# Shorter runs in the memory layout of scratch, weights and inputs: a cross-attention and mixture-of-experts block on one Trainium2 core

## The chip, the core and the metric

One Trainium2 chip, of which the kernel uses one core. The metric is the device time in microseconds of one execution; the time of a kernel is the median of several runs. The engines are called TensorE (PE; its weight loads are PEld), VectorE (DVE), ScalarE (ACT), GpSimd (POOL) and SyncE (SP). DMA transfers are issued here from two queues: SP's (q1 in the profile, "hardware_dynamic") and POOL's (q0, "software_dynamic"). Both run on the same 16 DMA engines of the core.

## What is computed

`x` is (4, 512, 512), `ctx_1024` is (4, 512, 256), all float32. A cross-attention whose queries and keys come from the context is added to `x`, then a transformer block with 16-head causal attention and a mixture of experts (16 experts of width 352, the best 6 for each token, and one shared expert of width 704).

```python
def _L0_xattn_ref(teacher_logits, teacher_features, Wq, bq, Wk, bk):
    query = jnp.einsum('bnc,dc->bnd', teacher_features, Wq) + bq
    key = jnp.einsum('bnc,dc->bnd', teacher_features, Wk) + bk
    energy = jnp.einsum('bnd,bmd->bnm', query, key)
    attention = jax.nn.softmax(energy, axis=-1)
    return jnp.einsum('bln,bmn->blm', teacher_logits, attention)
...
    h = rmsnorm(x, ln1_w)
    q, k, v = h @ wq, h @ wk, h @ wv          # 16 heads of 128
    attn = softmax(causal(q k^T / sqrt(128)))
    x = x + (attn v) @ wo
    t = rmsnorm(x, ln2_w)
    probs = softmax(t @ gate_w.T); topv, topi = top_k(probs, 6); topv = topv / sum(topv)
    hh = silu(t eg_w^T) * (t eu_w^T)          # each expert
    out = x + sum_e cw_e (hh ed_w^T) + shared expert(t)
...
x = x + _L0_xattn_ref(_layernorm(x), ctx_1024, ...)
x = x + _L0_ffn_ref(_layernorm(x), ...)
```

(The second block is shortened to its formulas.)

## The kernel before

Every float32 matrix is split into a high and a low float16 part, and a product is three matmuls (`mm3`, L80 to L87). A tile has 128 partitions (rows); tokens go in four tiles of 128 per batch element, called "batch" here.

The work has three stages. The head (`xattn`, L204) is the cross-attention of one batch. It runs for batch 0 first, then mostly for batch 1; batches 2 and 3 are advanced in small steps (`bring`) between the heads of the second stage. For batches 0 and 1 its inputs are loaded from SP's queue, for batches 2 and 3 from POOL's (`feed`, L176). Weights of head 0 (`wqk0`) and group 0 (`wv0`) are loaded early from SP (L221).

The second stage goes over 64 pairs of batch and attention head in the order of `path`: `queries`, `values` (once for two heads), `scores`, `attend` one head later (`LAG`), `project` after each pair of heads. `scores` turns the softmax's result with a DMA transpose on SP's queue (`flip`, L90 and L91): `pt<-pn`, four a head, 256 in all. `attend` reads `pt`. Similar transposes are `ptp<-pn` and `hT<-hh` in the cross-attention and `h2T<-h2p` before the router.

`fetch` (L407) brings the weights of a head (`wqk`) or of a group of two heads (`wv`, `wo`). The first time it loads float32 into a staging tile (L423), splits it, and stores the split weights to a scratch tensor in memory (L429). Two neighbouring batches share a fetched tile (`partner`); for the other pair of batches the tile is fetched back from scratch (L414). Scratch stores and fetches are on POOL's queue, apart from the first head's store.

Other rows go to memory and back. (The profile leaves numbers out of names, so `x1_d` is `x_d` there.) The cross-attention stores its result `x1_d` (L339) and, for batches 2 and 3, its normed rows `hid_d` (L356), which `project` loads (L698). `rest_step` (L522) and `last_residual` reload `x1_d`, add, and store the residual `r_d`, which `residual` (L709) loads as the accumulator `acc` on SP's queue. `shared_weights` (L440, load at L451) loads the shared expert's weights piece by piece. `pad_rows` (L479) fills rows of the token buffer `xs_d` with zeros, once for each of 16 experts. The routed tokens are scattered into `xs_d` with indirect DMAs on POOL's queue (L467).

The third stage runs the shared expert and then 16 experts on the gathered tokens, with their weights from SP's queue (L939), outputs in `y_d`, and indirect gathers (`yg`) that add them to `acc`.

The order of the instructions on each engine is made at build by a planner with a simulated timeline; `after` (L93) adds an order between two instructions, `pin` keeps program order. Within a queue, instructions go in that order; the program states no order between queues except through the data.

Of the kernel before, what the change touches and what calls it, by code (L numbers as in the profile page):

```python
# [47 lines left out]
PS = 4096.0  # L48
GS = 8.0
LAG = 1  # L50
MLAG = 2
# [4 lines left out]
def xattn_moe_block_kernel(ctx: ExitStack, tc: tile.TileContext, x, xT, ctxT, wqkx, bqk, ln1, ln2,  # L56
# [23 lines left out]
    def mm3(o, terms, start=True, stop=True, hold=None):  # L80
        n = len(terms)
        for j, (lh, ll, rh, rl) in enumerate(terms):
            ins = nc.tensor.matmul(o, lh, rh, start=start and j == 0, stop=False)  # L83
            if hold and j == 0:
                after(ins, hold)
            nc.tensor.matmul(o, lh, rl, start=False, stop=False)  # L86
            ins = nc.tensor.matmul(o, ll, rh, start=False, stop=stop and j == n - 1)  # L87
        return ins

    def flip(o, i):  # L90
# [40 lines left out]

    hid_d = [dram.tile([P, NT, D], F32, name=f"hid_d{b}") for b in range(B)]
    x1_d = [dram.tile([P, NT, D], F32, name=f"x1_d{b}") for b in range(B)]
    wqk_d = [dram.tile([P, 2048], F16, name=f"wqk_d{h}") for h in range(H)]
    wv_d = [dram.tile([P, 8 * GW], F16, name=f"wv_d{g}") for g in range(G)]
    wo_d = [dram.tile([P, 2 * HG * D], F16, name=f"wo_d{g}") for g in range(G)]
    xs_d = dram.tile([ROWS, 2 * D], F16, name="xs_d")
    r_d = [dram.tile([P, NT, D], F32, name=f"r_d{b}") for b in range(B)]
    y_d = dram.tile([OFFS[E], D], F32, name="y_d")
# [39 lines left out]
    def ctx_load(b):  # L179
        t = stg.tile([P, 1024], F32, tag="st", name="ct32").rearrange("p (c s) -> p c s", c=CC)  # L180
        feed(b).dma_start(t, ctxT[b])
        return t

# [20 lines left out]
    def xattn(b):  # L204
        ct32 = ctx_load(b) if b else ct0

        def turned(j):
            t = (stg if b else wg).tile([P, 1024], F32, tag="st" if b else "wo", name="xT32")
            feed(b).dma_start(t, xT[b, j])
            return t  # L210
# [5 lines left out]
        if b == 0:  # L216
            nc.sync.dma_start(ln1b, ln1.partition_broadcast(P))
            for nm, src in (("wqk0", wqk[0]), ("wv0", wv[0])):
                t = vp.tile([P, NT, 2, GW], F16, tag="vt", name=f"{nm}_st")
                early_st[nm] = t.rearrange("p t a d -> p (t a d)").bitcast(F32)  # L220
                nc.sync.dma_start(early_st[nm], src)  # L221
        ctp = ap_.tile([P, 2, CC, S], F16, tag="lnp", name="ctp")
# [109 lines left out]
        for t in range(NT):  # L332
# [5 lines left out]
            q = nc.gpsimd if b else nc.sync  # L338
            q.dma_start(x1_d[b][:, t, :], xv)  # L339
            st = asm.tile([P, 6], F32, name="st")  # L340
# [14 lines left out]
            if b >= 2:  # L355
                q.dma_start(hid_d[b][:, t, :], hd)  # L356
            if stop == "A":
# [36 lines left out]
    def shared_pool():  # L394
        actx.close()
        sp = ctx.enter_context(tc.tile_pool(name="sp", bufs=1, side="right", reuse_waits="tile"))
        shx["p"] = ctx.enter_context(tc.tile_pool(name="ac0", bufs=1, side="right", reuse_waits="tile"))
        shw = shx["w"] = sp.tile([P, 2, C * 2 * SI], F16, name="shw")
        sdw = shx["d"] = sp.tile([P, 2, 6 * D], F16, name="sdw")
        for j in range(0, C * 2 * SI, 1024):  # L400
            pieces.append((shw[:, :, j:min(j + 1024, C * 2 * SI)], sgu[:, j:min(j + 1024, C * 2 * SI)]))
        for j in range(0, 6 * D, 1024):
            pieces.append((sdw[:, :, j:j + 1024], sd[:, j:j + 1024]))

    held, partner, seen = {}, {}, set()

    def fetch(b, g, pool, tag, n, src, scr, nm):  # L407
# [5 lines left out]
        if nm in seen:  # L413
            nc.gpsimd.dma_start(w.rearrange("p a n -> p (a n)"), scr)  # L414
            return w
        seen.add(nm)
        first = nm in early_st
        if first:
            st_ = early_st[nm]
        else:  # L420
            st_ = stg.tile([P, 1024], F32, tag="st", name=f"{nm}_st")
            q = nc.sync if nm == "wqk1" else nc.gpsimd
            ins = q.dma_start(st_[:, :n], src)  # L423
            if nm == "wqk1":
                after(ins, zz["hT", 0])
        for j, ins in enumerate(split(w[:, 0], w[:, 1], st_[:, :n], WS)):
            if first:
                after(ins, zz["nb"] if j else zz["calm"][0])
        ins = (nc.sync if nm == "wqk0" else nc.gpsimd).dma_start(scr, w.rearrange("p a n -> p (a n)"))  # L429
        if nm != "wqk0":  # L430
# [9 lines left out]
    def shared_weights():  # L440
# [6 lines left out]
        if pieces:  # L447
            dst, src = pieces.pop(0)
            n = src.shape[1]
            st_ = stg.tile([P, 1024], F32, tag="st", name="shst")[:, :n]  # L450
            pin(nc.gpsimd.dma_start(st_, src))  # L451
            loaded.append((dst, st_))
# [26 lines left out]
    def pad_rows(e):  # L479
        r = e * T + CAP + 1 - 3 * HB  # L480
        dst = xs_d[r:r + 3 * HB, :].rearrange("r d -> (r d)").rearrange("(p a n) -> p a n", p=P, a=2)
        src = causal[:, :S - P].bitcast(F16).unsqueeze(1).to_broadcast([P, 2, 2 * (S - P)])
        after(nc.gpsimd.dma_start(dst, src), zz["pad"])

    def route1(b, x2):
# [20 lines left out]
        if b == B - 1:  # L506
            pace(h2p[0:1, D:D + 1])
            for t, x1t in enumerate(x1s):
                after(nc.gpsimd.tensor_tensor(x1t, x1t, x2[:, t, :], ALU.add), scats[0])
                nc.gpsimd.dma_start(r_d[b][:, t, :], x1t)  # L510

    x1s = []

    def last_residual(b):
        for t, (pool, tag) in enumerate([(he, "pn3"), (he, "pn3"), (xp, "x1t"), (xp, "h2")]):
            x1t = pool.tile([P, D], F32, tag=tag, name="x1t", **({} if pool is he else dict(bufs=1)))
            nc.gpsimd.dma_start(x1t, x1_d[b][:, t, :])
            x1s.append(x1t)
# [3 lines left out]
    def rest_step():  # L522
        if rest:
            b, t, x2 = rest.pop(0)
            x1t = xp.tile([P, D], F32, tag="x1t", name="x1t", bufs=1)
            ins = nc.gpsimd.dma_start(x1t, x1_d[b][:, t, :])
            for s in scats[-1:]:
                after(ins, s)
            nc.gpsimd.tensor_tensor(x1t, x1t, x2[:, t, :], ALU.add)
            nc.gpsimd.dma_start(r_d[b][:, t, :], x1t)  # L530

# [163 lines left out]
    def project(b, g):  # L695
        if b not in x2s:
            x2s[b] = x2p.tile([P, NT, D], F32, tag="x2", name="x2")
            nc.gpsimd.dma_start(x2s[b], hid_d[b])  # L698
        ao, x2 = aos[b, g], x2s[b]
# [9 lines left out]
    def residual(b):  # L709
        if b not in accs:  # L710
            pool = hpool if b else shx["p"]
            accs[b] = pool.tile([P, NT, D], F32, tag="hT", name=f"acc{b}")
            nc.sync.dma_start(accs[b], r_d[b])
        return accs[b]
# [522 lines left out]
def host_layout(i):  # L1237
# [5 lines left out]
    r["x"] = f["x"]  # L1243
    r["xT"] = f["x"].transpose(0, 2, 1).reshape(B, 2, 2, P, S).transpose(0, 1, 3, 2, 4).reshape(B, 2, P, 2 * S)
    r["ctxT"] = f["ctx_1024"].transpose(0, 2, 1).reshape(B, CC, P, S).transpose(0, 2, 1, 3)
    r["wqkx"] = np.stack([_pc(f["L0_xattn_Wq"].T, CC), _pc(f["L0_xattn_Wk"].T, CC)], 1)
# [6 lines left out]
    for n in ("wqk", "wv", "wo"):  # L1253
        r[n] = r[n].reshape(r[n].shape[0], P, -1)
    r["gate"] = _pc(g("gate_w").T, C).reshape(P, C * E)
# [10 lines left out]
    cols.append(np.concatenate([sg[:, :, 5 * P:], su[:, :, 5 * P:]], 2).reshape(P, C * P))  # L1266
    r["sgu"] = np.concatenate(cols, 1)
    r["sd"] = _pc(np.pad(g("sd_w").T, ((0, 6 * P - SI), (0, 0))), 6).reshape(P, 6 * D)
    return {k: np.ascontiguousarray(v) for k, v in r.items()}
# [24 lines left out]
```

## Time and profile before

| | |
|---|---|
| median of 3 runs | 1773.08 us (1766.79 to 1774.21) |
| profiled execution, its own time | 1762.41 us |
| its span, first to last instruction | 1760.7 us |
| mean granted TensorE clock | 0.993 |
| bytes moved by DMA | 296.24 MB, 168 GB/s over the span |
| memory read, written | 124.81 MB, 88.94 MB |
| `wqk<-wqk_d`, POOL, 20 times 512 KB | 5.0 us from issue to landing (median) |
| `wqk_d<-wqk`, POOL, 15 times 512 KB | 4.0 us |
| `wqk_st<-in_wqk_dram`, POOL, 14 times 512 KB | 6.4 us |
| `xs_d<-causal`, POOL, 16 times 384 KB | 5.6 us |

The profile is of one execution. Its busy shares are averages over the span; its line of DMA digits gives, in 40 equal slices, the mean busy share of the 16 DMA engines in tenths. A row of a DMA issue has the line, the issuing queue, what is written from what, how many, KB each, and the median time from issue to landing. The duration of an issue on POOL's queue is the time in which POOL prepares the transfer, not the transfer itself. A row of the window view has start and end, length, then the busy time of each engine with its instructions, the granted clock, the DMA share and GB/s. The rows of the DMA queues have packets, MB, and the time that their packets took as a share of 16 engines over the window; packets that overlap can bring a share over 100%. Under the profile lie the trace's packet records, each with its queue, start, duration and size.

### The profile page before, as it was taken

The numbers are of one execution on the slowest core, as the hardware profiler recorded it, in microseconds if no ns is written. First come the engines' busy times: TensorE is split into PE (matmuls) and PEld (weight loads), VectorE is DVE, ScalarE is ACT, GpSimd is POOL, SyncE is SP. The second block draws the span as 40 slices with busy tenths as digits, with TensorE's granted clock in tenths as the row PEclk, the third lists the DMA queues.
The fourth block names the chain that finished last, engine by engine and source line by source line (L and its number), as shares of the span: only waits on it lengthen the run. The fifth ranks groups of instructions, "written<-read, shape, count | busy, mean of one in ns | idle before, by whom it ended". The sixth has DMA issues, their size and how long they took to land. (4 is left out here: it accounts for less than half of the span.)

```text
span 1760.7 us, 27659 instructions
## 1 busy us (share of the span) xinstructions
PE 1708.6 (97%) x9919; PEld 932.9 (53%) x9919; DVE 1116.2 (63%) x2766; ACT 829.3 (47%) x1711; POOL 485.1 (28%) x614
## 2 busy tenths in 40 slices
PE   7899999999998999999999999999999999999998
PEld 3555556565654555556555544455555555555553
DVE  6787877787785676776667647544434344356755
ACT  4565655565643545454445422344544445444431
POOL 5524212240255242121113454300000000034654
PEclk9999999999999999999999999999999999999999
DMA  7787867575687787556547653755554546589866
GB/s 246 181 205 184 225 150 192 122 196 118 138 183 187 163 177 179 120 120 118 111 104 132 140 155 128 247 173 148 150 173 137 154 143 163 154 228 254 221 198 213
DMA packets 392212, 296.24 MB, mean 168 GB/s; under 512 B 334880, under 2 KB 335136, under 8 KB 391296
## 3 DMA queue, kind: packets, MB, share of 16 engines
q1 hardware_dynamic: 353360, 159.87, 39.9%
q0 software_dynamic: 38704, 134.51, 25.5%
q8 instruction: 80, 1.31, 0.3%
q14 instruction: 68, 0.56, 0.1%
HBM read 124.81 MB, written 88.94 MB: 121 GB/s over the span
## 5 line engine op out<-in xcount | busy, mean ns | idle before, releaser
L1169 POOL DMA_INDIRECT yg<-y_d,yrc x96 | 109.9, 1145 | 505.2 <-PE u L87 426.0
L673 ACT ACTIVATE pe<-pe,bnm 128x128 f32<-128x128 f32 (+3 forms) x256 | 142.5, 557 | 161.5 <-DVE bnm L671 161.3
L83 PE MATMUL qk<-hT,wqk 128*128 128x512 f16 (+1 forms) x520 | 196.4, 378 | 9.1 <-DMA wqk<-wqk_d 5.5
L86 PE MATMUL qk<-hT,wqk 128*128 128x512 f16 (+1 forms) x520 | 196.5, 378 | 0.0
L87 PE MATMUL qk<-hT,wqk 128*128 128x512 f16 (+1 forms) x520 | 196.3, 377 | 0.0
L74 DVE SCALAR_TENSOR_TENSOR pn<-pe,brc,pn 128x128 f16<-128x128 f32 (+3 forms) x256 | 148.1, 590 | 21.3 <-ACT pn L73 18.0
L671 DVE CUSTOM_DVE_ANT_0 pe<-sc,causal 128x128 f32<-128x128 f32 (+3 forms) x256 | 117.0, 485 | 66.9 <-PE sc L668 65.9
L73 ACT ACTIVATE pn<-pe,brc 128x128 f16<-128x128 f32 (+3 forms) x256 | 133.5, 553 | 34.1 <-ACT pe L673 17.8
L83 PE MATMUL v<-wv,hT 128*128 128x256 f16 x512 | 139.8, 273 | 0.9 <-DMA hT<-hh 0.9
L87 PE MATMUL v<-wv,hT 128*128 128x256 f16 x512 | 139.7, 273 | 0.0
L86 PE MATMUL v<-wv,hT 128*128 128x256 f16 x512 | 139.7, 273 | 0.0
L83 PE MATMUL g<-xT,wt 128*128 128x384 f16 (+2 forms) x384 | 127.3, 331 | 0.0
L86 PE MATMUL g<-xT,wt 128*128 128x384 f16 (+2 forms) x384 | 127.2, 331 | 0.0
L87 PE MATMUL g<-xT,wt 128*128 128x384 f16 (+2 forms) x384 | 127.2, 331 | 0.0
L1058 ACT ACTIVATE hT_e<-hf 128x384 f16<-128x384 f32 (+3 forms) x96 | 51.1, 532 | 133.6 <-DVE hf L1072 133.2
L83 PE MATMUL y<-dt,hT_e 128*128 128x512 f16 (+1 forms) x288 | 109.4, 380 | 0.0
L87 PE MATMUL y<-dt,hT_e 128*128 128x512 f16 (+1 forms) x288 | 108.9, 378 | 0.0
L86 PE MATMUL y<-dt,hT_e 128*128 128x512 f16 (+1 forms) x288 | 108.9, 378 | 0.0
L73 ACT ACTIVATE qkt<-qk 128x512 f16<-128x512 f32 x128 | 75.1, 587 | 70.7 <-PE qk L87 70.5
L705 DVE SCALAR_TENSOR_TENSOR x<-wo,x 128x512 f32<-128x512 f32 x128 | 87.2, 685 | 33.3 <-PE wo L87 32.9
L467 POOL DMA_INDIRECT xs_d<-h2p,slotu x96 | 98.7, 1028 | 28.3 <-issue 27.1
L74 DVE SCALAR_TENSOR_TENSOR qkt<-qk,qkt 128x512 f16<-128x512 f32 x128 | 87.5, 684 | 18.3 <-ACT qkt L73 15.2
(333 smaller groups left out, 4041.5 us busy)
## 6 DMA issues: line engine op xcount, KB each, us to landing
y_d<-yt SPq DMA_DIRECT2D x96, 256.0 KB, 2.8
est<-in_ew_dram SPq DMA_DIRECT2D x32, 704.0 KB, 6.2
est<-in_ed_dram SPq DMA_DIRECT2D x16, 768.0 KB, 4.7
wqk<-wqk_d POOLq DMA_DIRECT2D x20, 512.0 KB, 5.0
wqk_d<-wqk POOLq DMA_DIRECT2D x15, 512.0 KB, 4.0
wqk_st<-in_wqk_dram POOLq DMA_DIRECT2D x14, 512.0 KB, 6.4
xs_d<-causal POOLq DMA_DIRECT2D x16, 384.0 KB, 5.6
wv<-wv_d POOLq DMA_DIRECT2D x10, 512.0 KB, 5.7
```

Source lines behind the costliest of these rows:

```text
L73: return (nc.scalar.activation(hi, src, AF.Copy, scale=scale), nc.vector.scalar_tensor_tensor(lo, src, scale, hi, ALU.mult, ALU.subtract))
L74: nc.vector.scalar_tensor_tensor(lo, src, scale, hi, ALU.mult, ALU.subtract))
L83: ins = nc.tensor.matmul(o, lh, rh, start=start and j == 0, stop=False)
L86: nc.tensor.matmul(o, lh, rl, start=False, stop=False)
L87: ins = nc.tensor.matmul(o, ll, rh, start=False, stop=stop and j == n - 1)
L467: ins = nc.gpsimd.indirect_dma_start(out=xs_d, out_offset=bass.IndirectOffsetOnAxis(ap=slotu[:, tt, k:k + 1], axis=0), in_=h2ps[tt], in_of ...
L671: nc.vector.tensor_tensor_reduce(pe, ps[:, :w], causal[:, S - w:], -1.0, 3e38, ALU.add, ALU.min, nm)
L673: nc.scalar.activation(pe, pe, AF.Exp, bias=nm, scale=-1.0, accum_out=sm)
L705: nc.vector.scalar_tensor_tensor(x2[:, t, :], ps, 1.0 / (VS * WS), x2[:, t, :], ALU.mult, ALU.add)
L1058: nc.scalar.activation(hT[:R, ic, :w], hf, AF.Copy)
L1169: nc.gpsimd.indirect_dma_start(out=yg, out_offset=None, in_=src, in_offset=bass.IndirectOffsetOnAxis(ap=idx[:, tt, k:k + 1], axis=0))
```

## The change

A helper `runs` issues a DMA in which the side in memory is blocked: its outer index counts runs, then come 128 partitions, then the run itself, so that one partition's row is made of runs that lie apart, and the same run of the 128 partitions lies together. The tile on chip keeps its layout. With `RUN = 256` float32 (512 float16) the scratch of the split weights (`wqk_d`, `wv_d`, `wo_d`), of the residual (`x1_d`, `r_d`) and of the normed rows (`hid_d`) has runs of 1 KB. A partition's 4 KB of split weights were one run; a token tile's 2 KB of `x1_d`, `r_d` or `hid_d` were one run of a row of 8 KB. The inputs `xT`, `ctxT`, `wqk`, `wv`, `wo` and the shared expert's `sgu` and `sd` are laid out on the host in runs of 2 KB instead of 4 KB. `pad_rows` writes three runs of 1 KB a partition instead of two of 1.5 KB. Queues, waits, tiles and the work of the engines are the same in the program's text.

```diff
+RUN = 256
...
+    def runs(q, o, i):
+        blocks = [v.rearrange("p (q n) -> p q n", q=w.shape[0]) if len(v.shape) == 2 else v.rearrange("q p n -> p q n")
+                  for v, w in ((o, i), (i, o))]
+        return q.dma_start(*blocks)
...
-    hid_d = [dram.tile([P, NT, D], F32, name=f"hid_d{b}") for b in range(B)]
-    x1_d = [dram.tile([P, NT, D], F32, name=f"x1_d{b}") for b in range(B)]
-    wqk_d = [dram.tile([P, 2048], F16, name=f"wqk_d{h}") for h in range(H)]
-    wv_d = [dram.tile([P, 8 * GW], F16, name=f"wv_d{g}") for g in range(G)]
-    wo_d = [dram.tile([P, 2 * HG * D], F16, name=f"wo_d{g}") for g in range(G)]
+    def rows_d(nm, b):
+        return dram.tile([NT, D // RUN, P, RUN], F32, name=f"{nm}{b}")
+
+    def weights_d(nm, i):
+        return dram.tile([2048 // (2 * RUN), P, 2 * RUN], F16, name=f"{nm}{i}")
+
+    hid_d, x1_d, r_d = ([rows_d(nm, b) for b in range(B)] for nm in ("hid_d", "x1_d", "r_d"))
+    wqk_d = [weights_d("wqk_d", h) for h in range(H)]
+    wv_d, wo_d = ([weights_d(nm, g) for g in range(G)] for nm in ("wv_d", "wo_d"))
...
-        feed(b).dma_start(t, ctxT[b])
+        runs(feed(b), t, ctxT[b])
...
-            feed(b).dma_start(t, xT[b, j])
+            runs(feed(b), t, xT[b, j])
...
-                nc.sync.dma_start(early_st[nm], src)
+                runs(nc.sync, early_st[nm], src)
...
-            q.dma_start(x1_d[b][:, t, :], xv)
+            runs(q, x1_d[b][t], xv)
...
-                q.dma_start(hid_d[b][:, t, :], hd)
+                runs(q, hid_d[b][t], hd)
...
-            nc.gpsimd.dma_start(w.rearrange("p a n -> p (a n)"), scr)
+            runs(nc.gpsimd, w.rearrange("p a n -> p (a n)"), scr)
...
-            ins = q.dma_start(st_[:, :n], src)
+            ins = runs(q, st_[:, :n], src)
...
-        ins = (nc.sync if nm == "wqk0" else nc.gpsimd).dma_start(scr, w.rearrange("p a n -> p (a n)"))
+        ins = runs(nc.sync if nm == "wqk0" else nc.gpsimd, scr, w.rearrange("p a n -> p (a n)"))
...
-            pin(nc.gpsimd.dma_start(st_, src))
+            pin(runs(nc.gpsimd, st_, src))
...
-        dst = xs_d[r:r + 3 * HB, :].rearrange("r d -> (r d)").rearrange("(p a n) -> p a n", p=P, a=2)
-        src = causal[:, :S - P].bitcast(F16).unsqueeze(1).to_broadcast([P, 2, 2 * (S - P)])
+        dst = xs_d[r:r + 3 * HB, :].rearrange("r d -> (r d)").rearrange("(a p n) -> p a n", p=P, n=2 * RUN)
+        src = causal[:, :RUN].bitcast(F16).unsqueeze(1).to_broadcast([P, 3, 2 * RUN])
...
-                nc.gpsimd.dma_start(r_d[b][:, t, :], x1t)
+                runs(nc.gpsimd, r_d[b][t], x1t)
...
-            ins = nc.gpsimd.dma_start(x1t, x1_d[b][:, t, :])
+            ins = runs(nc.gpsimd, x1t, x1_d[b][t])
...
-            nc.gpsimd.dma_start(x2s[b], hid_d[b])
+            runs(nc.gpsimd, x2s[b].rearrange("p t d -> p (t d)"), hid_d[b].rearrange("t h p n -> (t h) p n"))
...
-            nc.sync.dma_start(accs[b], r_d[b])
+            runs(nc.sync, accs[b].rearrange("p t d -> p (t d)"), r_d[b].rearrange("t h p n -> (t h) p n"))
...
-        r[n] = r[n].reshape(r[n].shape[0], P, -1)
+        r[n] = r[n].reshape(r[n].shape[0], P, 2, -1).transpose(0, 2, 1, 3)
...
-    r["sgu"] = np.concatenate(cols, 1)
+    r["sgu"] = np.concatenate(cols, 1).reshape(P, -1, S).transpose(1, 0, 2)
```

## The prediction

> **What bounds the kernel now.** I read the page first, then what TensorE waits for, then the DMA traffic in the stretches where it waits, then the rows of the DMA issues that the change rewrites.
>
> ```profile
> span 1760.7 us, 27659 instructions
> ...
> PE 1708.6 (97%) x9919; PEld 932.9 (53%) x9919; DVE 1116.2 (63%) x2766; ACT 829.3 (47%) x1711; POOL 485.1 (28%) x614
> ...
> DMA  7787867575687787556547653755554546589866
> ...
> q1 hardware_dynamic: 353360, 159.87, 39.9%
> q0 software_dynamic: 38704, 134.51, 25.5%
> ```
>
> TensorE bounds it: 1760.7 - 1708.6 = 52 us of the span are free of matmuls. The change touches no matmul, so it can take at most these 52 us, and of them only what waits for DMA. The view of TensorE's waits says which:
>
> ```profile
> PE av L83 <- DMA pt<-pn: 16.9, 10, 3.9
> PE xm L83 <- DMA ptp<-pn: 9.8, 2, 5.8
> PE qk L83 <- DMA wqk<-wqk_d: 5.5, 1, 5.5
> PE u L1081 <- DVE hf L1072: 3.9, 2, 2.1
> PE qk L83 <- DMA hT<-hh: 3.6, 2, 3.2
> ```
>
> Columns are us in total, times, longest. DMA ends 37 us of waits (16.9 + 9.8 + 5.5 + 3.6 + 0.9), nearly all on transposes (`flip`, SP's queue, q1), which share the 16 DMA engines with the fetches and stores of POOL's queue (q0). In the timeline of TensorE, two belong to the head (5.8 us at 19.8, 3.2 us at 48.1) and twelve lie between 72 and 970 us: ten on `pt` (1.9, 2.5, 2.2 and 3.9 us, and six of 0.7 to 1.6), one on `ptp` (4.0 at 72.6) and the 5.5 us on a `wqk` fetch at 543. By the trace's packet records, q0 held 42% to 69% of the DMA engines in the 6 us before eleven of the twelve. A `pt` transpose lands after 2.3 us at best, 3.7 in the median, 10.8 at worst.
>
> So the question is what shorter runs do to the time that a q0 transfer holds the engines. A fetch almost alone, in windows of 4.3 and 3.9 us:
>
> ```profile
> q0 software_dynamic: 144, 0.52, 44.5%
> ...
> wo<-wo_d POOLq DMA_DIRECT2D x1, 512.0 KB, 4.2
> ```
>
> ```profile
> q0 software_dynamic: 80, 0.26, 23.1%
> ...
> x1t<-x_d POOLq DMA_DIRECT2D x1, 256.0 KB, 3.4
> ```
>
> The first, in rows of 4 KB, holds the engines 0.445 x 4.3 = 1.91 us. At the rate of the saturated head it would need 524 KB / 397 GB/s = 1.32 us:
>
> ```profile
> 15.00:20.00 5.00, 4.82 (x22) 1.95 (x20) 4.74 (x12) 5.00 (x11) 1.19 (x1) 1.00 1.04 397
> ```
>
> The missing 0.6 us is no cost per byte. The packet records show it at the start: the first 16 to 30 packets of such a fetch, one or two from each engine, take 300 to 1150 ns, nearly all later ones 159. All four quiet `wo` fetches (438, 688, 852, 907 us) look like this; quiet stores of 256 and 512 KB begin with packets of 156 to 260. So reads collide when 16 engines start together[...].
>
> **Part by part.**
>
> *Scratch of the split weights, 4 KB rows to 4 runs of 1 KB (40 fetches, 32 stores).* POOL's packets already join short runs: a fill of 256 runs of 1536 B appears as packets of 4608 B, 178 ns each, and row transfers of 2 KB as packets of 4096 B at 159 ns. So I expect the same packets, each made of four runs. The Trainium skill ("DMA: Bandwidth & Descriptors", Why small descriptors are slow) speaks against the change: every descriptor carries 32 B of metadata. Three more per packet are 96 B on 4096, 2.3%, or 0.03 us of a 1.32 us fetch. The trace has less: 4608 B in three runs moves at 25.9 B/ns, 4096 B in one at 25.8. I take zero, and keep the rule's 0.03 us x 72 = 2 us as a bound. The other effect is on the collision: [...]the four runs of a packet lying 128 KB apart. No row shows this pattern. Bounds: the whole 0.6 us gone, or 0.6 us more. The nearest row is `x1t`, runs of 2 KB: 0.231 x 3.9 = 0.90 us for 256 KB, so 0.24 us over its 0.66, against 0.30 us per 256 KB for `wo`: a fifth less from halving the run. But its runs lie 8 KB apart, so the reads spread over no less memory than before; the new runs are packed. I therefore lean to most of the 0.6 being gone, knowing that the row alone would give 0.12.
>
> *Issue on POOL.* More descriptors cost POOL time to write:
>
> ```profile
> L414 POOL DMA_DIRECT2D wqk<-wqk_d x20: 528/546/597, 444.0 to 958.8; - x20
> ```
>
> ```profile
> L215 POOL DMA_DIRECT2D xt<-in_x_dram x2: 788/812/837, 136.6 to 347.6; - x2
> ```
>
> The first writes 128 descriptors, the second 512: (812 - 546) / 384 = 0.7 ns each. The 71 scratch transfers on POOL gain 384 (+0.27 us, 19 us in all); 43 first loads and 52 row transfers gain 128 (+0.09, 8.5 us), two `hid_d` loads 896 (+0.62, 1.2 us), 16 fills 128 (+0.09, 1.4 us): 30 us of POOL's queue over 1000 us, where POOL has only 28% of the span in work. No wait of TensorE ends on POOL, so I cost it at nothing; behind a longer issue stand `mark`, the scatters and the norm steps of later batches, and without cover each is 0.27 us late. The skill ("SBUF — State Buffer", A bandwidth-pool intuition that's wrong) says that VectorE in its two-port mode locks GpSimd out of writing descriptors, 620 ns becoming 3100. By it, 71 issues could cost 2.5 us each. With VectorE busy 63% of the span, the 40 fetches issued in 527 to 597 ns: this mix does not show the trap, and I take the row.
>
> *Residual and norm rows (2 KB to 1 KB) and fills (1.5 KB to 1 KB).* Packets join as above: no change in engine time. Fills land with nobody waiting. On SP's queue runs are not joined (8 KB rows are packets of 309 ns in the records): `acc`, 8 KB to eight runs of 1 KB, would by the line through 84 ns (2 KB), 159 (4 KB) and 309 (8 KB) take 8 x 47 = 376 ns instead of 309, +0.5 us a load, four loads; `x1_d` stores of batch 0 take 0.08 us longer each, the one scratch store on SP (`wqk_d` of head 0) 0.2. TensorE waits for none of them: 0. Uncovered they are 2.7 us together.
>
> *First loads, 4 KB to 2 KB.* On POOL: joined, with a fifth of the collision gone at most by the `x1t` row. On SP it costs: before the first transposes the queue holds two `ct`, three `xT`, `wqk0` and `wv0`, 7 x 8 = 56 packets of 4 KB per engine, each becoming two of 84 instead of one of 159: 56 x 9 ns = 0.5 us. DMA is full from 5 to 25 us and TensorE waits 5.8 us there for `ptp`, so the 0.5 us is on the path. The start (first packets 720 ns, 257 GB/s from 4 to 6 us) may give some back; I count none.
>
> *Sum.* The nine waits after the first scratch fetch (393.5 us) each lose 0.6 us, 5.4; four of them (5.5, 2.5, 2.2, 3.9) are long enough for two fetches, an estimate, 2.4 more; the three earlier ones, behind 2 KB loads, 0.3 each, 0.9. Together -8.7, head +0.5: -8.2 us. The profiled execution itself took 1762.41 us, so 1754.2. The median of before, 1773.08, is 10.7 us longer than that execution; TensorE's work is fixed, so I take such runs to wait somewhat more for DMA, and round to -9: 1764. What is late next is the same `pt`, now behind transposes ahead of it on SP.
>
> **Rivals.**
>
> *Likeliest (0.48): the collision goes, 1764, own range 1754 to 1769.* For: 0.6 of 1.91 us sits in first packets, and TensorE's waits follow q0. Against: the 2 KB row gained little. With every one of the twelve waits gone it would be 1773 - 26 = 1747.
>
> *Neutral (0.28): the change does not do what it is built for.* Runs matter little; the collision comes from 16 engines starting at once. Then 0.12 us a fetch over twelve waits, 1.4, less 0.5, is 0.9: 1772. For: the `x1t` row; 97% of the span is matmuls.
>
> *Slower (0.24): packed 1 KB runs collide more.* If sixteen engines on neighbouring 1 KB runs, stepping 128 KB together, meet in fewer places of memory than on 4 KB rows, a fetch holds the engines 2.5 us instead of 1.91. Twelve waits grow by 0.6 us, 7; about as many transposes that now just arrive in time become late (an estimate), 7; with the head 15: 1788. It decides from about 2.3 us a fetch: 0.4 x 24 = 9 us. For: stalls of this size exist in every 4 KB fetch, and nothing shows that shorter runs cure them.
>
> Beside these, the build orders each engine's instructions by modelled DMA times; other descriptors may reorder some. No row prices it; I allow 3 us either way.
>
> **Numbers.** A measurement of this kernel can tell about 0.5% (9 us) from no change. The first case puts 0.40 under 1764.2 and 0.08 within; the second 0.26 within and 0.02 above; the third is above. Range 1753 to 1787: it leaves out the lowest tenth of the first case and somewhat under half of the third.
>
> **What would show it.** TensorE's count and busy time unchanged; q0's bytes unchanged and its share under 23% (25.5 now); a lone `wo` fetch near 1.4 us of engine time with its first packets near 159 ns; `pt` waits near 10 us, not 16.9; fetches issued in about 0.81 us on POOL; the `ptp` wait of the head 0.5 us longer. Wrong, if a fetch stays at 1.8 us or more, if q0's packets shrink to 1 KB, or if TensorE's order changes.

## The result, and the profile after

The changed kernel takes 1780.56 us in the median (1770.76 to 1792.87, 18 runs); the kernel before, run beside it, 1769.32 us (1753.3 to 1784.13, 18 runs). The ratio is 1.0083, 95% interval 1.0059 to 1.0107: the change makes the kernel slower by 0.8%, about 15 us (the medians alone lie 11 us apart). The forecast was 9 us faster.

The page of the changed kernel, profiled in an execution of 1774.86 us. The lines answer to those shown of before:

```profile
span 1773.1 us, 27663 instructions
...
PE 1712.6 (97%) x9919; PEld 932.8 (53%) x9919; DVE 1122.2 (63%) x2766; ACT 831.1 (47%) x1711; POOL 518.3 (29%) x614
...
DMA  8796876667578767565436643865564545589866
...
q1 hardware_dynamic: 358992, 159.87, 40.2%
q0 software_dynamic: 38960, 134.51, 25.1%
```

The bytes and the count of matmuls are those of before. POOL has 33 us more to do (485.1 before), nearly all of it in issuing. The share of q0 hardly fell (25.5% before), and its packet count hardly rose, so short runs are still joined into packets of 4 KB. TensorE is free for 1773.1 - 1712.6 = 60.5 us, 8.4 more than before. And it is busy 4 us longer with the same matmuls, much of which fits its granted clock (see the end of experiment 4 and the last section). TensorE's waits in the changed kernel (us in total, times, longest):

```profile
PE av L84 <- DMA pt<-pn: 24.1, 13, 6.3
PE xm L84 <- DMA ptp<-pn: 13.9, 3, 6.7
PE qk L84 <- DMA wqk<-wqk_d: 2.6, 1, 2.6
PE qk L84 <- DMA hT<-hh: 2.4, 2, 1.9
```

The same four names wait as before. `pt` grew from 16.9 to 24.1 us where 10 was forecast, `ptp` from 9.8 to 13.9. Two of the waits in the timeline of TensorE (start, duration, then in brackets the idle time before it):

```profile
27.47 0.59 PE L84 MATMUL xm<-ptp,lnp 128*128 128x512 f16 x1 [6.66 <-DMA ptp<-pn]
...
202.87 0.59 PE L84 MATMUL av<-pt,vt 128*128 128x512 f16 x1 [6.29 <-DMA pt<-pn]
```

The first is the head, 5.8 us before. The second stands at a place where the planner put another order: by tiles and shapes in the trace, 566 of 9919 matmuls, 269 of VectorE's and 11 of POOL's instructions stand elsewhere than in before. So a first question was whether layout or order made the loss.

What the change does to a single fetch is seen in a `wo` fetch that is almost alone. Both windows are 4.3 us long and begin with the issue on POOL; a digit of the DMA line is 0.11 us and counts a packet's whole time in the slice in which the packet starts. First the kernel before, then the changed kernel:

```profile
DMA  0000005983069990255968999974842300000000
```

```profile
DMA  0000006982000790797000386998999954403000
...
q0 software_dynamic: 144, 0.52, 39.1%
```

The digits 5983 and 698 at the left are a transpose of q1. Then comes the fetch. After, it begins two slices later (its issue on POOL is 0.22 us longer), and its last packets start five slices later, 0.5 us. The zeros in its middle are no idleness: by the packet records 31% to 35% of the engines' time is in use there for 0.3 us, where in before all of it is. It holds the engines 0.391 x 4.3 = 1.68 us, instead of 1.91. That looks like a gain, but it is none that can be told: fetches that were left as they were differ as much from kernel to kernel. Two more such windows of 4.3 us, first of a fetch as in before (1.52 us; kernel "stores in four" of experiment 4), then of one in eight runs (2.00 us; "fetches in eight"):

```profile
q0 software_dynamic: 144, 0.52, 35.3%
```

```profile
q0 software_dynamic: 144, 0.52, 46.5%
```

### The profile page after: what moved, and what is told of

Read it like the earlier page. It is cut to its first block, busy times and chain, and to the rows that moved or that the text cites. A ratio compares the mean times of both kernels' runs of the same rounds, so it can differ in the third digit from the quotient of the medians.

```text
span 1773.1 us, 27663 instructions
## 1 busy us (share of the span) xinstructions
PE 1712.6 (97%) x9919; PEld 932.8 (53%) x9919; DVE 1122.2 (63%) x2766; ACT 831.1 (47%) x1711; POOL 518.3 (29%) x614
## 3 DMA queue, kind: packets, MB, share of 16 engines
q0 software_dynamic: 38960, 134.51, 25.1%
```

## The experiments

Since the planner chooses a new order for nearly every edit, an order had to be held fixed. In all kernels below but the last of the section, an order is written into the kernel, that of before (in one kernel of experiment 1 that of the changed kernel): each engine's instructions are listed, and an order without a semaphore is added between neighbours. By the tiles in the traces, all 9919 matmuls of the kernels with before's order then stand as in before. The order that is written in costs nothing by itself: three such kernels of experiments 2 to 4 took 0.9974, 0.9982 and 1.0013 of before.

```diff
+def _freeze(nc, tc):
...
+            if last is not None:
+                tc.add_manual_dep(i, last.name, mybir.DependencyInfo(mybir.DependencyClass.NoSync, mybir.DependencyReason.DATA), reason="order")
+            last = i
```

Ratios are to runs of before on the same chip, with 95% intervals.

**1. Layout or order.** The whole new layout in the order of before; then the old layout in the order of the changed kernel.

> The whole new layout, but every engine keeps the instruction order of the kernel before (an explicit order between neighbours on each engine). Theory L, the layout itself costs: the first transposes of the head land 1 to 2 us later and a scratch fetch lands 0.3 to 0.5 us later, so the time stays as long as the changed kernel's, 8 to 15 us over before (1.005 to 1.009). Theory O, the other order that the planner chose costs: within 3 us of before, and the 6.3 us wait for pt at 196 us, where TensorE's order first differs, is gone.

> The old layout with the instruction order of the changed kernel on each engine. Theory L: within 3 us of before. Theory O: 8 to 15 us over before, with a wait of some 6 us for pt near 190 us. If both add, 4 to 8 us here and the same in the kernel with the layout alone.

Measured: layout alone 1.0088 (1.0058 to 1.0118), order alone 1.0026 (1.0004 to 1.0048). The layout carries the loss. The order that the planner found for it costs something on the old layout and nothing that can be seen on the new one (1.0083 with it, 1.0088 without).

**2. Which part of the layout.** First loads alone in runs of 2 KB; scratch of the split weights alone in runs of 1 KB; rows and fills alone in runs of 1 KB. Each is the matching part of the change's diff.

> Only the first loads in runs of 2 KB, order of before. Theory L puts part of the loss here: on SP's queue these runs become packets of 2 KB, the wait for ptp in the head grows from 5.8 to 6.5 us or more: 1 to 3 us over before. Theory O: 0 to 1 us.

> Only the scratch of the split weights in runs of 1 KB, order of before. Theory L: POOL prepares a transfer for 0.77 us instead of 0.55 and the engines run dry between its packets, a lone wo fetch takes 2.6 us instead of 2.3 from its first to its last packet: 3 to 8 us over before. Theory O: within 2 us. The prediction's first case: 5 us or more under before, since a lone fetch holds the engines for 1.6 us instead of 1.9.

> Only the residual and norm rows and the fills in runs of 1 KB, order of before. By the parts measured so far (scratch 0.56%, first loads 0.22%, all together 0.88%) 0.1% is left for these: within 0.3% of before under both theories.

Measured: loads 1.0022 (0.9997 to 1.0047), scratch 1.0056 (1.0032 to 1.008), rows and fills 0.9982 (0.9959 to 1.0005). The scratch is the main part; the loads may cost a little; the rows cost nothing.

**3. Addresses, number of runs, or POOL's time.** The scratch again in four runs of 1 KB, but each partition's runs beside each other in memory with a gap of 256 B, so that the addresses lie nearly as before (a partition every 5 KB, not 4):

```diff
-    wqk_d = [dram.tile([2048 // (2 * RUN), P, 2 * RUN], F16, name=f"wqk_d{h}") for h in range(H)]
+    wqk_d = [dram.tile([P, 4, 640], F16, name=f"wqk_d{h}")[:, :, :512] for h in range(H)]
```

> Scratch of the split weights in four runs of 1 KB a partition, but each partition's runs stay together in memory (a pitch of 1280 bytes, partitions 5 KB apart). Order of before. As many descriptors as in the kernel with packed scratch alone, which took 1.0056 of before; the addresses are near those of before. Theory D, the number of descriptors that POOL writes costs: 1.004 to 1.008 again. Theory A, the addresses cost (the same run of all partitions packed, one partition's runs 128 KB apart): within 0.25% of before.

Then the packed scratch in two runs of 2 KB, or eight of 512 B:

```diff
-    wqk_d = [dram.tile([2048 // (2 * RUN), P, 2 * RUN], F16, name=f"wqk_d{h}") for h in range(H)]
+    wqk_d = [dram.tile([2, P, 1024], F16, name=f"wqk_d{h}") for h in range(H)]
```

> Scratch in two packed runs of 2 KB a partition, order of before. Theory D: between before and the 1 KB scratch, near 1.003, since POOL writes 256 descriptors in place of 512. Theory A: between them too, if the loss grows with the number of places; if POOL's time for an issue (0.73 us for two runs, 0.77 for four, 0.55 for one) sets the loss, 1.004 to 1.005.

> Only the scratch of the split weights, now in 8 packed runs of 512 B per partition instead of 4 of 1 KB or 2 of 2 KB (measured 1.0056 and 1.0014), instruction order of before. Theory 'price rises with the number of runs': 1.009 to 1.015, issue on POOL above 0.85 us, pt waits above 25 us. Theory 'a threshold between 2 KB and 1 KB, above which the number of runs matters no more': 1.005 to 1.007.

And the old layout with one tiny instruction on POOL ahead of each transfer, which takes POOL's time and leaves the transfer as it was:

```diff
-            nc.gpsimd.dma_start(w.rearrange("p a n -> p (a n)"), scr)
+            busy = nc.gpsimd.memset(w[0:1, 0, 0:1], 0.0)
+            ins = nc.gpsimd.dma_start(w.rearrange("p a n -> p (a n)"), scr)
```

> The old layout, with one small extra instruction on POOL ahead of 70 of the 71 scratch transfers of its queue (a memset of one element of the tile to be fetched, which the fetch overwrites, or a copy of one element of the stored tile into the spent staging tile), 0.2 to 0.5 us each with what lies around it. Otherwise the order of before. It takes POOL's time as the longer issues do, with no more descriptors. If POOL's time alone makes the loss: 1.004 to 1.008 or more. If it is the descriptors behind the issue or the addresses: within 0.25% of before.

Measured: padded 1.0058 (1.0033 to 1.0083), two runs 1.0014 (0.9991 to 1.0037), eight runs 1.016 (1.0117 to 1.0204), POOL's time 0.9974 (0.9946 to 1.0002). Padded costs as much as packed, so the addresses are not what costs. POOL's timeline of that last kernel shows what was added:

```profile
444.90 0.09 POOL L439 MEMSET wqk<- 1x1 f16 x1 [5.19 <-PE qk L112]
445.29 0.53 POOL L440 DMA_DIRECT2D wqk<-wqk_d  x1 [0.30 <-POOL wqk L439]
```

This issue starts 0.39 us later, and the 40 fetches in the mean 0.50 us (the stores 0.24 us). Four runs lengthen an issue by 0.22 us. So each transfer is put off by as much or more, and the kernel is not slower.

**4. Fetch or store.** On the old layout, only one side moves in four (then eight) runs. They are taken from the last to the first on both sides, so that the data lands where it did and the runs can't be merged in the program. For the fetches in four runs:

```diff
-            nc.gpsimd.dma_start(w.rearrange("p a n -> p (a n)"), scr)
+            nc.gpsimd.dma_start(w.rearrange("p a n -> p (a n)").rearrange("p (q n) -> p q n", q=4)[:, ::-1], scr.rearrange("p (q n) -> p q n", q=4)[:, ::-1])
```

> The kernel before in its own instruction order, with one edit: the 40 fetches of split weights from scratch (20 wqk, 10 wv, 10 wo) go in 4 runs of 1 KB per partition, taken from the last to the first on both sides so that they can't be joined by the program; the scratch itself stays one piece of 4 KB per partition and the 32 stores stay single runs. Whole scratch in 4 runs cost 0.56% (1.0056 packed, 1.0058 padded). Theory 'the loss lies in the number of runs of the fetches, because the fetched weight comes later and its packets lie longer beside the transposes': 1.0045 to 1.006, waits of TensorE on pt 20 to 26 us. Theory 'each transfer pays alike': 40 of 72 transfers, so 1.003. Theory 'the loss lies in the stores': 1.000 to 1.001, pt waits as before (15 to 19 us).

> The mirror of the fetch-only kernel: the 32 stores of split weights into scratch (31 on POOL, one on SP) in 4 runs of 1 KB per partition, last to first on both sides, the 40 fetches single runs. Theory 'fetches': 1.000 to 1.001 and pt waits as before. Theory 'each transfer pays alike': 1.0025. Theory 'stores': 1.0045 to 1.006. If the two halves together come to much less than 1.0056, it is not the number of runs in the instruction but their being apart in address on one side that costs.

> Order and layout of before; all 40 fetches of split weights in 8 runs of 512 B per partition (last to first on both sides), stores as before. Theory 'the fetches lose, and the more runs the more': 1.008 to 1.014, more than the halves (1.0005 and 1.0026) add up to. Theory 'the halves add up': 1.002 to 1.004, and then the 0.57% of 4 runs was high by the scatter between calls, and the 1.6% of the packed 8-run scratch lies in the stores or in the addresses.

> The mirror: the 32 stores of split weights in 8 runs of 512 B per partition, fetches as before. The stores in 4 runs cost 1.0013. Theory 'fetches': 1.000 to 1.003. Theory 'at 512 B the stores lose too, before 430 us, where the first loads, the stores and the transposes lie together': 1.006 to 1.013.

Measured: fetches in four runs 1.0057 (1.0035 to 1.0078), stores in four 1.0013 (0.999 to 1.0036); fetches in eight 1.0048 (1.002 to 1.0075), stores in eight 1.0104 (1.0061 to 1.0148). At 1 KB the loss is the fetches', and at 512 B they lose no more; a loss of the stores is clear only at 512 B. By these, the 1.6% of the packed scratch in eight runs is 0.5% fetches and 1.0% stores, and it was wrong to read a price rising with the number of runs from it.

All these kernels issue the same matmuls in the same order, so the time between two given matmuls can be compared from trace to trace. The cuts are the starts of matmuls 0, 2400, 3600, 5200 and 5600, at 1.7, 429.1, 630.8, 886.3 and 950.8 us of before; nearly all stores lie in the first stretch, and the second has the densest fetches.

| kernel | runs in a fetch / a store | to 2400 | to 3600 | to 5200 | to 5600 |
|---|---|---|---|---|---|
| before | 1 / 1 | 427.4 | 201.8 | 255.5 | 64.4 |
| loads only | 1 / 1 | 435.6 | 202.4 | 253.5 | 66.1 |
| rows and fills only | 1 / 1 | 434.7 | 196.8 | 250.8 | 64.9 |
| POOL's time | 1 / 1 | 428.5 | 206.2 | 253.0 | 64.9 |
| stores in 4 | 1 / 4 | 432.8 | 195.2 | 251.9 | 64.6 |
| stores in 8 | 1 / 8 | 447.6 | 196.0 | 253.7 | 64.4 |
| scratch in 2 | 2 / 2 | 442.8 | 204.2 | 252.0 | 65.0 |
| scratch in 4, packed | 4 / 4 | 434.1 | 205.0 | 254.4 | 67.5 |
| scratch in 4, padded | 4 / 4 | 437.8 | 208.2 | 252.0 | 66.1 |
| whole layout | 4 / 4 | 433.6 | 211.9 | 253.3 | 68.2 |
| fetches in 4 | 4 / 1 | 430.1 | 210.2 | 255.5 | 65.2 |
| fetches in 8 | 8 / 1 | 424.4 | 209.0 | 254.2 | 68.0 |
| scratch in 8, packed | 8 / 8 | 454.0 | 207.5 | 254.4 | 68.9 |

Each number is of one profiled execution, and one alone says little: such a stretch scatters by some us. Together they are plain. In the second stretch the six kernels with fetches in one run take 199.7 us in the mean (standard deviation 4.4), the six with fetches in four or eight 208.6 (2.4): 8.9 us more, 0.5% of the kernel, about the loss measured. The last stretch has 2.4 us more, the third 0.9, within its scatter. In the first, only the two kernels with stores in eight runs stand clear, 448 and 454 against 424 to 438 (two runs, at 442.8, is not slower in its runs). The second stretch in the view by windows (start and end, length, busy time of each engine, granted clock, DMA share, GB/s), for stores in four, then fetches in four:

```profile
434.50:629.70 195.20, 189.76 (x1202) 108.19 (x1201) 144.57 (x413) 97.36 (x234) 82.56 (x116) 1.00 0.74 169
```

```profile
431.80:642.00 210.20, 194.29 (x1203) 109.49 (x1202) 144.81 (x413) 97.51 (x234) 86.73 (x116) 0.97 0.73 156
```

TensorE is idle for 15.9 us instead of 5.4, and busy 4.5 us longer with the same matmuls, at a granted clock of 0.97. These two lie near the ends of their groups; between the means of the groups it is 6.4 us of idle time and 2.5 us of slower matmuls. Two waits stand out in it. One is for `wqk` itself; TensorE in before, then with fetches in eight:

```profile
548.81 0.61 PE L83 MATMUL qk<-hT,wqk 128*128 128x512 f16 x1 [5.51 <-DMA wqk<-wqk_d]
```

```profile
550.30 0.61 PE L104 MATMUL qk<-hT,wqk 128*128 128x512 f16 x1 [7.43 <-DMA wqk<-wqk_d]
```

From matmul to matmul, this step takes 5.9, 8.5, 3.1, 7.3, 2.7 and 3.1 us in the six kernels with one run, and 6.0, 7.5, 7.0, 7.5, 7.8 and 7.4 in the six with more. The other is for a transpose that lies between two fetches; before, then the packed scratch in four:

```profile
585.43 0.39 PE L83 MATMUL av<-pt,vt 128*128 128x512 f16 x1 [2.48 <-DMA pt<-pn]
```

```profile
593.93 0.61 PE L104 MATMUL av<-pt,vt 128*128 128x512 f16 x1 [4.54 <-DMA pt<-pn]
594.33 0.63 PE L107 MATMUL av<-pt,vt 128*128 128x512 f16 x1
```

The matmul after the longer wait is the same instruction and takes 0.61 us instead of 0.39. This step takes 2.9, 1.5, 1.8, 2.7, 1.4 and 1.3 us in the six kernels with one run, and 4.9, 6.1, 4.7, 1.5, 4.8 and 2.7 in the six with more: longer in four of them.

The packet records say what lies behind. The mean landing of all 256 `pt` transposes hardly differs (3.76 us in before, 3.58 with stores in four, 3.81 with fetches in four, 3.75 with fetches in eight). In the second stretch, with its 51 transposes and 12 to 14 fetches, it does. There the fetches land after 4.4 to 5.3 us in the means of the six kernels with one run, and after 5.6 to 6.1 us in the six with more. The transposes land after 3.74 us (3.48 to 4.02) against 4.05 us (3.88 to 4.11), and 2 to 7 of them need over 6 us, against 6 to 11. So in this stretch a fetch in several runs lands about 1 us later, and the transposes beside it come later too.

A fetch that is alone is held up much less. Means in us, from the start of its issue, over fetches with no other transfer of POOL's queue and hardly any of SP's beside them:

| runs in a fetch | kernels, fetches | issue on POOL | first packet | last packet ends | engine time | packets over 250 ns, of 128 |
|---|---|---|---|---|---|---|
| 1 | 8, 39 | 0.56 | 1.26 to 1.28 | 3.47 to 3.65 | 1.65 to 1.91 | 15 to 23 |
| 2, packed | 1, 6 | 0.74 | 1.45 | 3.72 | 1.74 | 17 |
| 4, not packed | 2, 9 | 0.79 | 1.50 | 3.76 to 3.80 | 1.71 to 1.78 | 16 to 19 |
| 4, packed | 3, 15 | 0.78 to 0.79 | 1.50 | 4.04 to 4.15 | 1.64 to 1.78 | 14 |
| 8, not packed | 1, 5 | 0.93 | 1.66 | 4.15 | 1.90 | 18 |
| 8, packed | 1, 5 | 0.92 | 1.64 | 4.51 | 1.81 | 13 |

From the end of the issue to the first packet it is 0.7 us in every row, so the longer issue is all of the later beginning. The dip in the middle (fewer than 8 engines at work, for 0.1 to 0.2 us in the mean) is found in the packed fetches alone, and these land 0.3 us later than the others with as many runs. Yet kernels with packed and unpacked fetches lose alike (1.0056, and 1.0058 and 1.0057), so the dip is not what costs. The time for which the engines are held does not follow the number of runs.

With stores in eight a long wait for a transpose stands in the first stretch:

```profile
109.46 0.59 PE L104 MATMUL av<-pt,vt 128*128 128x512 f16 x1 [7.59 <-DMA pt<-pn]
```

In before there is no wait at that matmul (its place is 99.6 us there). But a wait of 6.2 us stands there with the scratch in two too, which is not slower in its runs, so this one wait does not prove where the stores lose.

**5. Which fetches.** Eight runs for the 20 fetches of `wqk` alone, then for the 20 of `wv` and `wo` alone.

```diff
-            nc.gpsimd.dma_start(w.rearrange("p a n -> p (a n)"), scr)
+            o, i = w.rearrange("p a n -> p (a n)"), scr
+            if nm.startswith("wqk"):
+                o, i = (v.rearrange("p (q n) -> p q n", q=8)[:, ::-1] for v in (o, i))
+            nc.gpsimd.dma_start(o, i)
```

> Order and layout of before; only the 20 fetches of split wqk go in 8 runs of 512 B per partition (last to first on both sides), to have a large effect: the whole scratch in 8 runs cost 1.6%. Theory 'the loss comes at the few places where TensorE waits for a transpose or for wqk itself beside a fetch of wqk (549 and 585 us of before)': 1.009 to 1.014, and most of what the two kernels of this call lose together. Theory 'late wv and wo': 1.000 to 1.004. Alike by number: 1.007 to 1.008 each.

> The mirror: only the 10 fetches of split wv and the 10 of split wo in 8 runs of 512 B per partition, wqk as before. Theory 'tight places beside wqk': 1.001 to 1.005. Theory 'late wv and wo': 1.009 to 1.014. Alike by number: 1.007 to 1.008 each.

Measured: `wqk` 1.0005 (0.9983 to 1.0028), `wv` and `wo` 1.0026 (1.0002 to 1.005). Neither theory foretold so little of both. Together it is 0.3%, within the intervals of the 0.48% of all fetches in eight; which half carries more can't be told. In the one trace of each, `wqk` alone has the long step to the matmul that waits for `wqk` (7.6 us) and no loss in its runs; `wv` and `wo` alone have 0.6 us at that step, but 10.9 us at the step that waits for `pt`. So neither wait is the loss by itself.

**6. Late, or in the way.** Is it enough that the weights land later? On the old layout POOL clears 1024, then 2048 elements of the tile before each fetch:

```diff
-            nc.gpsimd.dma_start(w.rearrange("p a n -> p (a n)"), scr)
+            busy = nc.gpsimd.memset(w[0:1, 0, :1024], 0.0)
+            ins = nc.gpsimd.dma_start(w.rearrange("p a n -> p (a n)"), scr)
```

> Layout and order of before; ahead of each of the 40 fetches of split weights POOL first clears 1024 elements of one partition of the tile that the fetch then fills, so that each fetch starts later, an estimate of 1 us (a single element cost 0.09 us and a gap of 0.30 before the issue). With 4 or 8 runs the fetches landed 0.3 to 1.0 us later than before in mean. Theory 'lateness alone': 1.004 to 1.007, as with fetches in 4 or 8 runs (1.0057, 1.0048), TensorE's wait on wqk near 550 us above 7 us. Theory 'the descriptors lie in the way of the transposes': 0.999 to 1.002.

> The same with 2048 elements, each fetch about twice as late. Theory 'lateness alone': 1.007 to 1.013, above the first. Theory 'descriptors': 1.000 to 1.004, a wait for the weights themselves only.

Measured: 1.0045 (1.0011 to 1.0078) and 1.0015 (0.9985 to 1.0044). The longer delay, from the tile's rows of that kernel, and its wait for `wqk`:

```profile
L439 POOL MEMSET wqk<- x20: 1794/1794/1795, 453.6 to 969.0; 1x2048 f16 x20
```

```profile
PE qk L108 <- DMA wqk<-wqk_d: 4.8, 1, 4.8
```

Each fetch is issued 2.1 us later (1.79 and a gap of 0.30 or more), 1.3 us with the shorter delay, far more than four runs delay it. Yet the second stretch takes 199.7 us (197.8 with the shorter delay), the wait for `wqk` is no longer than before, and the 51 transposes of that stretch land after 3.26 and 3.48 us, sooner than in before (4.02). So starting late does not make the loss of that stretch. The time of the shorter delay, 1.0045, lies where lateness alone was to put it, and the longer one, which was to cost more, does not show it; in the trace of the shorter one it is the last stretch that is long (68.3 us), and whether that is more than scatter is open. This speaks against lateness alone, and for something that a fetch in several runs does while it lies beside the transposes. It does not prove the second, since a late start also moves a fetch to another place among them.

**7. The part that did not lose, as one would ship it.** Rows and fills only, with the planner free.

> The part of the change that did not lose, as one would ship it: residual and norm rows and the fills in runs of 1 KB, everything else as before, and the planner free to choose its own order (with the order of before it measured 0.9982, interval 0.9959 to 1.0005). If the rows help by themselves: 0.996 to 0.999. If the planner's new order takes back what rows give (its order for the whole change cost 0.26% on the old layout): 1.000 to 1.002.

Measured: 1.0076 (1.005 to 1.0101), where the same layout in the order of before gave 0.9982. The planner's order alone takes 0.9%, 17 us, more than any part of the layout but the stores in eight. It has a wait that is not in before's list:

```profile
PE wo L84 <- ACT ao L74: 5.8, 1, 5.8
```

So no kernel was found that is surely faster than before.

## Why the prediction was wrong

**What bounds the kernel: right.** TensorE's matmuls are the span, and the rest is mostly waits for `pt`, `ptp`, `wqk` and `hT`. But a wait was priced at its length. The granted clock falls to half for 3.4 or 6.8 us in or just after long waits (in before at 25, 52, 76, 547 and 970 us), so the wait at 585 us in the packed scratch cost its 2.1 us more and then the slower matmuls.

**Scratch, the collision: the step that failed.** The prediction took most of 0.6 us a fetch as gone, where its only row for shorter runs, `x1t`, gave 0.12. No such gain can be seen. Lone fetches hold the engines 1.64 us in the changed kernel, in the mean, and 1.64 to 1.78 us in all kernels with four runs; in kernels whose fetches were left as they were it is 1.65 to 1.91. The 1.91 that the sum started from is the highest of these means: in one execution its scatter could not be seen. The slow first packets are still there, 14 to 19 of 128 over 250 ns with four runs, 15 to 23 with one. So there was nothing to turn into shorter waits, and the waits for `pt` rose.

A second term was mis-sized. The four runs of a packet were taken as free: zero, with a bound of 2 us by the price of descriptor bytes. The fetches alone measured 0.57%, some 10 us. What the runs show in place of the gain is that in the stretch with the densest fetches a fetch in several runs lands about 1 us later, and the transposes with it 0.3 us later (experiment 4). The packet rate of 25.9 against 25.8 B/ns that stood behind the zero was measured in a fill, which nobody waits for and which does not read memory; it says nothing on how soon a read's packets come.

**Issue on POOL: right.** The issue of a scratch transfer takes 0.77 us (0.81 forecast, from 0.546):

```profile
L94 POOL DMA_DIRECT2D wqk<-wqk_d x20: 751/770/817, 463.6 to 975.8; - x20
```

POOL's 33 us (30 forecast) cost nothing that can be seen: the fetches 0.50 us later and the stores 0.24 us gave 0.9974. The trap of VectorE's two-port mode, an estimate of 2.5 us an issue from the 620 and 3100 ns of the Trainium skill ("SBUF — State Buffer", A bandwidth-pool intuition that's wrong), does not show here either: the 20 `wqk` fetches took 751 to 817 ns.

**Rows and fills: right**, at 0 (0.9982, with an interval that reaches 1.0005). **First loads:** +0.5 us was forecast for the head. Its `ptp` wait rose from 5.8 to 6.7 us, and to 6.4 with the loads alone; but it lies between 5.0 and 6.6 us in traces with the old loads, and is 5.7 with the whole layout in before's order, so this rise is not certain. The loads alone measured +0.2%, 4 us, not certain either. **Order:** "3 us either way" was too narrow for this planner: 0.26% in one case, 0.9% in another. In this change it did not decide.

**The sum.** -9 us was forecast and +15 measured. The parts measured by themselves give 0.57% for the fetches, 0.13% for the stores, 0.22% for the loads and -0.18% for the rows, 0.74% together, against 0.88% (0.58 to 1.18) for the whole layout.

**The rivals.** The slower one had the right side, and its 1788 was nearer than the 1764, by a wrong mechanism: it let packed runs hold the engines 2.5 us, but they hold them 1.64 to 1.78, and the unpacked fetches in four lose as much. That its number is near is luck. The neutral one had the collision right (shorter runs do little to it) and put no price on the runs. Of the signs written down, q0's share (25.1%, not under 23), the engine time and first packets of a lone fetch, and the `pt` waits (24.1 us, not near 10) all told against the likeliest case, and TensorE's order did change. But "wrong, if a fetch stays at 1.8 us or more" was not met at 1.68: by itself that test would have passed a change that lost, since fetches that were left alone lie on both sides of 1.8 too.

**What stays open.** That the number of runs in a fetch costs the 0.5% is shown, and that fetches and transposes of the second stretch land later in those kernels is seen in the traces. How they hold each other up is not shown. Nor is it shown on which side two runs stand (1.0014; second stretch 204.2 us, between the groups). That POOL's descriptors come too slowly for 16 engines is no good explanation of the dip in a lone fetch, since unpacked fetches with as many runs have none; what makes the dip is open.

## What to carry to other kernels

Ask of a transfer when it lands, and who has no slack for it, before asking how long it holds the engines: here the hold did not change and the kernel lost 0.5%. And look at the same transfer in several kernels that leave it alone before believing a difference of two traces. Keep what is fetched on demand in long runs (2 KB was not surely worse than 4 KB here, 1 KB was), above all in stretches where a transpose on another queue is on the path. And where a planner orders the instructions, freeze the order before judging a part of a change, since the order alone moved this kernel by as much as the change did.

## What had not been expected of the hardware

- TensorE at half clock after a wait: granted 0.50 for 3.41 or 6.83 us at a time (10.24 us four times, 13.65 us once, in all traces). In all it is at half clock for 27.7 us in before, 33.5 in the changed kernel and up to 59.8 us (packed scratch in eight), 7.2, 6.2 and 5.2 of them at the very end. The Trainium skill ("TensorE: Matmul & The Clock Gate", What's actually happening) names a window of 3413 ns; the lengths in these traces are that and its multiples.
- A `pt` transpose lands after about 2.3 us plus 0.9 to 1.0 us for each us of q0's engine time that falls into it, by a line through the packet records of each of seven traces; alone it takes 2.3 us in the mean, beside more than 2.5 us of q0 5.8 to 6.4. (A transpose that is late for another reason also collects more of q0's time.)
- The first packet of a fetch from memory on POOL's queue starts 0.7 us after the issue has ended, whatever its number of runs; the issue takes 0.56 us with one run a partition, 0.74 with two, 0.79 with four, 0.93 with eight.
- Runs of 512 B in a store to memory cost 1.0% in 32 stores of 512 KB, runs of 1 KB about nothing; in 40 fetches 1 KB already costs the 0.5%, and 512 B no more (1.0104, 1.0013, 1.0057 and 1.0048).
